# Moving the setup of four second-half rows from the start of a kernel into its groups 2 to 4, with new priorities for the first half

## The chip, the cores and the metric

The kernel runs on one core of one Trainium2 chip. A core has five engines that run side by side: TensorE for matrix products (PE in the profile, PEld for its weight loads), VectorE (DVE), ScalarE (ACT), GpSimd (POOL), and SyncE (SP), whose only work here is to issue DMAs. The metric is the device time of one launch in microseconds (us). The kernel before was run three times, and its median is 2317.83 us (2316.39 to 2319.93).

## What is computed

The input x holds 128 samples of 64 tokens with 512 features, and adj a 64 by 64 matrix for each sample. Four layers follow one another. Each is `x = x + f(relu(layernorm(x)), adj)`, all in float32. The four f, cut to what matters here:

```python
# layer 0: hypergraph convolution, twice, with layer norm between
h = relu(Dn * H @ (Be * H.T @ (x @ W1.T)) + b1);  h = layer_norm(h, gamma, beta)
y = Dn * H @ (Be * H.T @ (h @ W2.T)) + b2 + x
# layer 1: s = (x @ w) @ a decides the attention weights
A = exp(leaky(8 * tanh((s_i + s_j) / 8))) * adj;  y = normalised(A) @ x @ w
# layer 2: query and key with biases, value
y = normalised(adj * exp((x @ Wq.T + bq) @ (x @ Wk.T + bk).T)) @ (x @ Wv.T + bv)
# layer 3: two scores per token, then three powers of a transition matrix
Xw = X @ Wv + bv;  sj = Xw @ aw[:512];  si = Xw @ aw[512:]
T = rownormalised(adj * exp(leaky_relu(sj_j + si_i + ab)))
y = relu(sum over k of (T^k X @ Wk[k] + bk[k]))
```

Two small results of weights alone matter for the change. The first is the column `gb_c`, Wk transposed times bq, which layer 2 adds to its queries. The second is the pair of rows `c3_b[:, s, :]`, Wv times one half of aw, with which layer 3 takes its two scores straight from the normalised x, and with them the scalar `kap` (bv times both halves of aw, plus ab). No layer of the first half reads any of these.

## The kernel before, in words

The 8192 tokens are cut into NG = 16 groups of 512, and a group into four tiles of 128 tokens. The **first half** of the kernel takes every group through layers 0 and 1 (`layer0`, L771; `layer1`, L849) and stores x to DRAM. The **second half** loads it again and takes every group through layers 2 and 3 (`layer2`, L896; `layer3`, L1009). The large products are Strassen products of two by two blocks (`strassen` at L673 and `chained` at L621), so DVE, ACT and POOL have block sums to make between the matmuls. Weights are combined once (`combine` at L395), at the start for the first half, and at the joint of the halves for the second.

The order of the work is not written out. Each step is entered into a `Graph` (L40) with an engine, a cost and a priority, and `Graph.run` (L84) plays the whole program through once with these costs and gives each engine its list of instructions. It takes on each engine the step that can start first, and among steps that can start at the same time the one with the lowest priority number. The number is `G.prio + G.shift`: `G.prio` begins at g * PERIOD1 in the first half, or 16 * PERIOD1 + g * PERIOD2 in the second, and grows along the layer by `step`, stretched by `STRETCH`. `G.shift` is the entry of the table `AT` (L291) for the part named by `part(...)`. So a lower number means earlier, and only differences count. The entries end00, end01 and end11 are added for the last groups: end01 for layer 1 of group 14, end11 for layer 1 of group 15. When the graph foresees over 1 us of idle time on PE, `fill` (L1195) puts in matmuls of `ones` with no use for their result, for half of that time. They are on L1199 in the profile.

Buffers are slots of a tag. A step that needs a new buffer waits until a slot of the tag is free. The tag `tmp` has four slots of 128 by 512, and three kinds of work use it:

- the setup: `setup_l2` (L469, products of Wq and Wk), `setup_l1` (L463, the row `wa_b` for layer 1), `setup_bq` (L486) and `setup_l3` (L503), through `temp` (L341) with its load on L338;
- `spread` (L455), which turns a column into a row on all partitions: a DVE product on L458, a matmul with ones on L460, an ACT copy on L461;
- `transposed` (L597) in layer 0: an ACT copy into a slot (L601), a DMA transpose (L602), and an ACT copy of what came back (L603).

Several tags of the first half hand their memory to tags of the second half once all their steps are done (`TWO`, L197): the block sums `s2` and `s1` to `zz`, `wa` to `q`, `z` to `hT`, `mT` to `sx`.

Before, `setup_bq` and `setup_l3` are entered at the start, after the combinations of the first half's weights. `setup_bq` loads four blocks of Wk, sums them with the entries of bq on DVE (L492, L494), and takes a matmul with ones (L499) and a copy (L501). `setup_l3` does for each s two broadcast loads (aw and bv3) and four loads of Wv, five dot products on DVE (`dot`, L390, on L392), and one `spread`; two small additions (L514, L515) make `kap`. All DMAs are on SP's queue, in one order.

Of the kernel before, what the change touches and what calls it, by code (L numbers as in the profile page):

```python
# [14 lines left out]
P = 128  # L15
C = 64
D = 512
# [154 lines left out]
def tile_adj_preln_d4(  # L172
# [111 lines left out]
    def quad(b):  # L284
# [2 lines left out]
    FILL, LAT = 0.5, 2.3  # L287


    STRETCH, PERIOD1, PERIOD2 = (2.4057, 23.1237, 14.6194, 5.0478), 88.385, 152.83  # L290
    AT = {  # L291
        "x0": -4649.81, "apart": 515.41, "w1": 891.32, "b1": 147.15, "w2": 1055.04, "w": 146.66, "c1": 74.0, "l0":
        181.27, "c2": 131.25, "l1": 1241.14, "c": -4314.2, "g0": -2118.58, "g1": -4213.04, "g2": -574.45, "g3":
        -1827.82, "g": -443.79, "bq": -420.39, "l3": -143.58, "wg": 627.97, "wp": 228.79, "beg0": -1054.79, "beg1":
        -138.73, "end00": 1.09, "end01": -86.62, "end11": 256.44, "new2": -124.9, "new3": 81.75, "end2": -68.63,
        "end3": -133.99, "load1": -63.98, "load2": 661.26, "m": -63.44, "h0": 2.91, "p0": 25.16, "z0": -386.05,
        "q0": 47.65, "y0": -4107.25, "h1": -19.07, "p1": 5.7, "z1": -84.16, "q1": 20.96, "y1": -130.14, "s": -234.6,
        "t0": -462.0, "e0": -467.09, "t1": -348.17, "e1": -282.93, "hT": 524.3, "sh": 245.53, "lq": 730.58, "pt":
        -113.04, "v": 589.88, "pv": 1100.8, "s3": 672.72, "tt": 1008.78, "a0": 690.15, "b0": 538.95, "a1": 811.73,
        "ws": 2002.18, "load3": 441.07, "bk": 299.55,  # L300
    }

    def part(name):
        G.shift = AT[name]
# [28 lines left out]
        dma(8, lambda: nc.sync.dma_start(sb, src), [], [name])  # L333
        return sb

    def load_tmp(tag, n, shape_of, src):
        b = Buf(tag)
        dma(n * P * 4 / 1024, lambda: nc.sync.dma_start(shape_of(b.t), src), [], [b])  # L338
        return b

    def temp(src):  # L341

        return load_tmp("tmp", D, lambda t: t, src)

    xt, adjs, xmid, rows = {}, {}, {}, []

# [136 lines left out]
            act(0.6, lambda c=c, e=e: nc.scalar.copy(e.t, ps[c].t), [ps[c]], [e])  # L483
            dma(256, lambda c=c, e=e: nc.sync.dma_start(wg_d[c * P:(c + 1) * P, :], e.t), [e], ["wg_d"])

    def setup_bq():  # L486

        pg, bk = Buf("ps"), Buf("o")
        for o in range(KD):
            k_ = temp(Wk[o * P:(o + 1) * P, :])  # L490
            if o == 0:
                dvp(0.45, lambda k_=k_: nc.vector.tensor_scalar(bk.t, k_.t, bq_c[:, 0:1], None, op0=ALU.mult), [k_, "bq_c"], [bk])  # L492
            else:
                dvp(0.85, lambda o=o, k_=k_: nc.vector.scalar_tensor_tensor(bk.t, k_.t, bq_c[:, o:o + 1], bk.t, op0=ALU.mult, op1=ALU.add),  # L494
                    [k_, "bq_c", bk], [bk])

        def mg():
            for c in range(KD):
                nc.tensor.matmul(pg.t[:, c:c + 1], bk.t[:, c * P:(c + 1) * P], ones[:, 0:1], start=True, stop=True)  # L499
        pe(c_mm(1, KD), mg, [bk], [pg])  # L500
        dve(0.2, lambda: nc.vector.tensor_copy(gb_c, pg.t[:, :KD]), [pg], ["gb"])  # L501

    def setup_l3():  # L503
        kk = Buf("mv")
        ab_t = load_tmp("rs", 1, lambda t: t, ab.partition_broadcast(P))
        for s in range(2):
            av, cc = temp(aw[s * D:(s + 1) * D].partition_broadcast(P)), Buf("col")
            bv_t = temp(bv3.partition_broadcast(P))
            dot(lambda bv_t=bv_t: bv_t.t, lambda av=av: av.t, lambda s=s: kk.t[:, s:s + 1], [bv_t, av], [(kk, s)])
            for c in range(KD):  # L510
                wv = temp(Wv3[c * P:(c + 1) * P, :])
                dot(lambda wv=wv: wv.t, lambda av=av: av.t, lambda c=c, cc=cc: cc.t[:, c:c + 1], [wv, av], [(cc, c)])
            spread(lambda cc=cc: cc.t, lambda s=s: c3_b[:, s, :], [(cc, c) for c in range(KD)], ("c3", s))
        dve(0.15, lambda: nc.vector.tensor_add(kap, kk.t[:, 0:1], kk.t[:, 1:2]), [(kk, 0), (kk, 1)], ["kap"])  # L514
        dve(0.15, lambda: nc.vector.tensor_add(kap, kap, ab_t.t), ["kap", ab_t], ["kap"])  # L515

# [492 lines left out]
    def layer3(g):  # L1009
# [66 lines left out]


        part("b0")
        sx = Buf("sx")
        keys = lambda i, v: [(a3[2 * i + v], n) for n in range(3)]  # L1080
        block = lambda i, j: [(lambda v=v: a3[2 * i + v].t[:, :, 2 * j:2 * j + 2, :]) for v in range(2)]
# [131 lines left out]
    setup_l1()  # L1213
    part("c")
    W = combine(wm, w_sb, w_x, 2, D // 2, "DVE")
    part("bq")
    setup_bq()
    part("l3")
    setup_l3()
    for g in range(NG):  # L1220
        G.prio = g * PERIOD1
        if g:
            part("load1")
            load_group(g, x_in)
        for i, layer in ((0, layer0), (1, layer1)):
            stretch[0] = STRETCH[i]
            if g == 0:
                G.prio += AT["beg0" if i == 0 else "beg1"]
            if i == 0 and g == NG - 1:
                G.prio += AT["end00"]  # L1230
            if i == 1 and g >= NG - 2:
                G.prio += AT["end01" if g == NG - 2 else "end11"]
            layer(g)
        G.prio = g * PERIOD1
        part("wp")
        if g:
            for k in range(2):
                if 2 * g - 2 + k < 21:
                    setup_w3(2 * g - 2 + k, [("z", g - 1 + k, 1 - k)], [("z", g, k)])
# [83 lines left out]
```

## Time and profile before

| | us |
|---|---|
| median of three runs | 2317.83 |
| lowest and highest | 2316.39, 2319.93 |
| the profiled execution, its own time | 2321.51 |
| its span, first to last instruction | 2319.7 |
| first matmul of layer 0 (L790) starts | 6.28 |
| first product of layer 1 (L691 with 256 columns on mT) starts | 149.68 |
| last product of layer 1 ends | 1223.6 |
| first product of layer 3 (L1124) starts | 1264.30 |

The granted TensorE clock is 0.999 of full speed over the whole execution. Times within the profile count from the span's first instruction. A timeline row has the start, the time from the first to the last of a run of equal instructions, the engine, line and operation, what is written and read, and in brackets the idle time before it with what ended it. A row of a table by stage has the busy time of each engine in a stretch, its instruction count in brackets, the granted clock, the busy share of the DMA engines and the rate of their transfers. A row of waits says which engine's instruction waited for which, for how long in total, how often, and the longest.

### The profile page before, as it was taken

Reading aid. Unit: us, or ns where it says so; the run is one execution under the profiler, and the core shown is the slowest. Engines: PE = TensorE matmul, PEld = TensorE weight load, DVE = VectorE, ACT = ScalarE, POOL = GpSimd, SP = SyncE. Lnnn points to the kernel's source line nnn. Section 1 sums busy time; section 2 is a strip of 40 time slices with the busy share of each in tenths; the row PEclk is TensorE's granted clock in tenths of the full one; section 3 lists DMA queues with packets and bytes.
Section 4 is the critical chain, followed back from the end, with each engine's and each line's share of the span. In section 5 each row is a group of like instructions: output and inputs, shape, how many; then the busy total and the mean of one; then the engine's idle time right before and its main releaser. Section 6 shows DMA issues by size and latency. Waiting matters only on the chain.

```text
span 2319.7 us, 39752 instructions
## 1 busy us (share of the span) xinstructions
PE 2279.9 (98%) x14238; PEld 1866.4 (80%) x14238; DVE 1865.1 (80%) x4004; ACT 1393.2 (60%) x1993; POOL 1190.9 (51%) x1771
## 2 busy tenths in 40 slices
PE   8999999999999999999999999999999999999998
PEld 4676677776777767777688999999999989999898
DVE  7887877887778877787867888888888878788787
ACT  4766565675655765656657566566656655656542
POOL 7445556545665465543433455545455544545443
PEclk9999999999999999999999999999999999999999
DMA  6443233443333342323436877787787877878767
GB/s 232 103 104 77 78 98 79 102 90 79 83 91 94 90 90 58 74 71 68 97 98 161 223 222 229 234 223 213 226 244 213 235 215 217 222 224 225 200 200 242
DMA packets 403478, 355.12 MB, mean 153 GB/s; under 512 B 290896, under 2 KB 321872, under 8 KB 403280
## 3 DMA queue, kind: packets, MB, share of 16 engines
q1 hardware_dynamic: 403280, 352.58, 55.5%
q8 instruction: 112, 1.84, 0.3%
q14 instruction: 86, 0.70, 0.1%
HBM read 241.05 MB, written 44.33 MB: 123 GB/s over the span
## 4 chain that ended last, share of the span: by engine, by line
PE 84%; DMA 6%; DVE 5%; ACT 3%; issue 1%; POOL 1%; SPq 0%; DVEq 0%; ACTq 0%; POOLq 0%
PE ps L691 38%; PE ps L1124 19%; PE ps L930 15%; PE ps L592 4%; PE ps L844 2%; PE ps L1067 2%; DMA w2m_wm_a_wf<-fac 1%; DMA h<-o 1%; PE ps L999 1%; PE ps L961 1%; DMA x<-xm 1%; DMA z_hT<-tmp_mB_xi 1%; ACT h L583 1%; DVE st L562 1%; DMA tmp_mB_xi<-in_Wk_dram 0%
## 5 line engine op out<-in xcount | busy, mean ns | idle before, releaser
L583 ACT ACTIVATE h<-x,nm,rs 128x512 f32<-128x512 f32 x384 | 306.2, 812 | 234.9 <-POOL nm L570 220.3
L564 POOL TENSOR_SCALAR rs<-mv 128x1 f32<-128x1 f32 x320 | 104.6, 327 | 388.4 <-DVE mv L563 371.1
L1124 PE MATMUL ps<-w2m_wm_a_wf 128*128 128x128 f32 x2256 | 295.5, 277 | 3.8 <-DMA w2m_wm_a_wf<-fac 2.2
L1124 PEld LDWEIGHTS ps<-w2m_wm_a_wf 128*128 128x128 f32 x2256 | 275.8, 192 | 11.1 <-issue 4.0
L691 PE MATMUL ps<-w2m_wm_a_wf,s_s_zz 128*128 128x256 f32 x1152 | 274.8, 380 | 1.8 <-DVE s_s_zz L683 1.8
L1124 PE MATMUL ps<-w2m_wm_a_wf,tmp_mB_xi 128*128 128x128 f32 x1968 | 260.4, 277 | 9.8 <-DMA w2m_wm_a_wf<-fac 5.2
L1124 PEld LDWEIGHTS ps<-w2m_wm_a_wf,tmp_mB_xi 128*128 128x128 f32 x1968 | 243.2, 193 | 16.6 <-ACT h L583 7.5
L691 PEld LDWEIGHTS ps<-w2m_wm_a_wf,s_s_zz 128*128 128x128 f32 x1152 | 217.7, 190 | 39.7 <-issue 9.6
L691 PE MATMUL ps<-w2m_wm_a_wf,rT_vu_tt 128*128 128x256 f32 x1024 | 237.5, 380 | 2.0 <-ACT row_sh L453 0.7
L691 PE MATMUL ps<-wa_mem,mT_sx 128*128 128x512 f32 x512 | 238.1, 593 | 1.3 <-DMA wa_mem<-in_W1T_dram 1.0
L691 PEld LDWEIGHTS ps<-w2m_wm_a_wf,rT_vu_tt 128*128 128x128 f32 x1024 | 193.6, 190 | 48.5 <-issue 18.4
L565 POOL TENSOR_TENSOR rs<-rs,mhalf 128x1 f32<-128x1 f32 x320 | 209.2, 654 | 26.5
L562 DVE BATCH_NORM_STATS2 st<-x 128x6 f32<-128x512 f32 x256 | 176.1, 688 | 33.0 <-DMA x<-xm 25.7
L570 POOL TENSOR_SCALAR nm<-mv,rs 128x1 f32<-128x1 f32 x320 | 171.4, 537 | 30.2
L691 PE MATMUL ps<-wa_mem,s_s_zz 128*128 128x512 f32 x384 | 180.3, 593 | 0.0
L691 PEld LDWEIGHTS ps<-wa_mem,mT_sx 128*128 128x128 f32 x512 | 96.0, 191 | 103.9 <-issue 97.9
L818 ACT ACTIVATE z_hT<-z_hT 128x512 f32<-128x512 f32 x128 | 79.3, 630 | 133.6 <-DVE z_hT L711 133.6
L603 ACT COPY rT_vu_tt<-z_hT 128x1024 uint16<-128x1024 uint16 x128 | 146.7, 1162 | 16.6 <-DMA z_hT<-tmp_mB_xi 16.5
L719 POOL TENSOR_TENSOR u<-u,row_sh 128x256 f32<-128x256 f32 x96 | 75.4, 794 | 157.3 <-DVE u L661 134.7
L592 PEld LDWEIGHTS ps<-bd,h 128*128 128x128 f32 x1024 | 126.6, 192 | 36.4 <-issue 27.6
L885 POOL TENSOR_TENSOR x<-x,u 128x256 f32<-128x256 f32 x96 | 88.8, 950 | 113.0 <-DVE u L663 113.0
L601 ACT COPY o<-h 128x1024 uint16<-128x1024 uint16 x128 | 133.8, 1047 | 9.3 <-DVE h L1056 6.9
(205 smaller groups left out, 4991.8 us busy)
## 6 DMA issues: line engine op xcount, KB each, us to landing
w2m_wm_a_wf<-fac SPq DMA_DIRECT2D x110, 768.0 KB, 5.0
w2m_wm_a_wf<-fac SPq DMA_DIRECT2D x109, 576.0 KB, 4.8
x<-xm SPq DMA_DIRECT2D x128, 256.0 KB, 3.5
x<-in_x_dram SPq DMA_DIRECT2D x64, 256.0 KB, 2.8
xm<-x SPq DMA_DIRECT2D x64, 256.0 KB, 2.0
out_dram<-x SPq DMA_DIRECT2D x64, 256.0 KB, 3.9
adj<-in_adj_dram SPq DMA_DIRECT2D x32, 256.0 KB, 4.6
fac<-wp_bv_bk SPq DMA_DIRECT2D x63, 128.0 KB, 2.0
```

The lines of the kernel that those rows point to most:

```text
L562: dve(0.69, lambda i=i: nc.vector.bn_stats(st.t[:, i, :], src(i)), [r[i]], [(st, i)])
L564: small(0.28, lambda: nc.gpsimd.tensor_scalar_add(rs.t, mv.t[:, 1:2], EPS), [mv], [rs])
L565: small(0.62, lambda: nc.gpsimd.tensor_tensor(rs.t, rs.t, mhalf, ALU.pow), [rs], [rs])
L570: small(0.32, lambda: nc.gpsimd.tensor_scalar(nm.t, mv.t[:, 0:1], rs.t, -1.0, op0=ALU.mult, op1=ALU.mult), [mv, rs], [nm])
L583: act(0.82, lambda: nc.scalar.activation(h.t, xx.t, AF.Relu, bias=nm.t, scale=rs.t), [xx, nm, rs], [h])
L592: nc.tensor.matmul(quad(p)[:, c, :], h.t[:, c * P:(c + 1) * P], rhs(), start=True, stop=True)
L601: act(1.05, lambda: nc.scalar.copy(u16(planes.t).rearrange("p (q c) -> p q c", q=2), u16(src()).rearrange("p (c q) -> p q c", q=2)), ksrc, ...
L603: act(1.16, lambda: nc.scalar.copy(u16(dst()).rearrange("p c (k q) -> p c k q", q=2), u16(back()).rearrange("p (q c r) -> p c r q", q=2, c ...
L691: nc.tensor.matmul(p.t[:, :n], lhs()[:, c, :], rhs(c), start=first and c == 0, stop=c == kc - 1, skip_group_check=True)
L885: pool(0.78, lambda: nc.gpsimd.tensor_add(xx.t[:, cols], xx.t[:, cols], U.t[:, iu]), [xx, u], [xx])
L930: nc.tensor.matmul(pair(p.t)[:, o, :], a, b, start=first and o == 0 and c == 0, stop=c == 1, skip_group_check=True)
L1124: nc.tensor.matmul(inner(p, q)[:, r, :], at()[:, k, :], wv()[:, r, k, :], start=first and r == 0 and k == 0, stop=k == 2, skip_group_check ...
```

## The change

`setup_bq` and `setup_l3` are no longer called at the start. They are called in the loop over the groups of the first half, after the layers of the group are entered: `setup_bq` in group 2, and the two halves of `setup_l3` in groups 3 and 4. Their loads get one more entry in their list of reads, `("z", g, 0)`. This names the last step of the layer norm of the first pair of tiles in layer 0 of that group (the `offset` on L570). It stands for no memory: the graph alone knows it, and the built program has no semaphore for it. Between groups 3 and 4 one slot of `mv` and one of `rs` (each has ten) stay taken, for the sums of `kap`.

STRETCH of layers 0 and 1, PERIOD1, and most of the entries in `AT` for the setup and the first half have new values. Those that belong to the second half (new2, new3, end2, end3, load2, hT, sh, lq, pt, v, pv, s3, tt, a0, b0, a1, ws, load3, bk, and wg) are the same. Two new entries, late3 and last3, are added to the priority in layer 3 of the last two groups; both are 0.

```diff
-    STRETCH, PERIOD1, PERIOD2 = (2.4057, 23.1237, 14.6194, 5.0478), 88.385, 152.83
+    STRETCH, PERIOD1, PERIOD2 = (2.5476, 23.631, 14.6194, 5.0478), 89.881, 152.83
     AT = {
-        "x0": -4649.81, "apart": 515.41, "w1": 891.32, "b1": 147.15, "w2": 1055.04, "w": 146.66, "c1": 74.0, "l0":
-        181.27, "c2": 131.25, "l1": 1241.14, "c": -4314.2, "g0": -2118.58, "g1": -4213.04, "g2": -574.45, "g3":
-        -1827.82, "g": -443.79, "bq": -420.39, "l3": -143.58, "wg": 627.97, "wp": 228.79, "beg0": -1054.79, "beg1":
-        -138.73, "end00": 1.09, "end01": -86.62, "end11": 256.44, "new2": -124.9, "new3": 81.75, "end2": -68.63,
+        "x0": -3955.4, "apart": 260.05, "w1": 1321.68, "b1": 557.01, "w2": 2258.25, "w": 829.09, "c1": -850.87,
+        "l0": -579.26, "c2": 1820.29, "l1": 854.76, "c": 115.55, "g0": -2147.26, "g1": -2547.69, "g2": -40.9, "g3":
+        -1911.72, "g": -569.47, "bq": 23.11, "l3": -4.68, "wg": 627.97, "wp": 228.79, "beg0": -1894.5, "beg1":
+        -468.39, "end00": -12.24, "end01": -489.71, "end11": 597.53, "new2": -124.9, "new3": 81.75, "end2": -68.63,
...
-    def load_tmp(tag, n, shape_of, src):
+    def load_tmp(tag, n, shape_of, src, r=()):
         b = Buf(tag)
-        dma(n * P * 4 / 1024, lambda: nc.sync.dma_start(shape_of(b.t), src), [], [b])
+        dma(n * P * 4 / 1024, lambda: nc.sync.dma_start(shape_of(b.t), src), r, [b])
...
-    def setup_bq():
+    def setup_bq(when):
...
-            k_ = temp(Wk[o * P:(o + 1) * P, :])
+            k_ = temp(Wk[o * P:(o + 1) * P, :], when)
...
-    def setup_l3():
-        kk = Buf("mv")
-        ab_t = load_tmp("rs", 1, lambda t: t, ab.partition_broadcast(P))
-        for s in range(2):
...
+    def setup_l3(s, when):
+        if not s:
+            sums.append((Buf("mv"), load_tmp("rs", 1, lambda t: t, ab.partition_broadcast(P), when)))
+        kk, ab_t = sums[0]
+        av, cc = temp(aw[s * D:(s + 1) * D].partition_broadcast(P), when), Buf("col")
+        bv_t = temp(bv3.partition_broadcast(P), when)
+        dot(lambda: bv_t.t, lambda: av.t, lambda: kk.t[:, s:s + 1], [bv_t, av], [(kk, s)])
+        for c in range(KD):
+            wv = temp(Wv3[c * P:(c + 1) * P, :], when)
+            dot(lambda wv=wv: wv.t, lambda: av.t, lambda c=c: cc.t[:, c:c + 1], [wv, av], [(cc, c)])
+        spread(lambda: cc.t, lambda: c3_b[:, s, :], [(cc, c) for c in range(KD)], ("c3", s))
+        if not s:
+            return
...
-    part("bq")
-    setup_bq()
-    part("l3")
-    setup_l3()
+    sums = []
     for g in range(NG):
...
+        if g in (2, 3, 4):
+            part("bq" if g == 2 else "l3")
+            when = [("z", g, 0)]
+            setup_bq(when) if g == 2 else setup_l3(g - 3, when)
+            part("wp")
```

## Prediction

> **What bounds the kernel now.** I read the page first, then busy time by stage, then TensorE's timeline where a stage shows idle time, then the waits there. The page:
>
> ```profile
> span 2319.7 us, 39752 instructions
> PE 2279.9 (98%) x14238; PEld 1866.4 (80%) x14238; DVE 1865.1 (80%) x4004; ACT 1393.2 (60%) x1993; POOL 1190.9 (51%) x1771
> ```
>
> TensorE is the bound, and 2319.7 - 2279.9 = 39.8 us is all it is idle. Its products are the same before and after, so the time can change by idle time and by the filler matmuls on L1199, which count as busy and are not work. Stages of 58 us show where that is (the second column is PE's busy time; the rows are the first four, one from the steady part, and three at the joint of the halves):
>
> ```profile
> 0.00:58.00 58.00, 51.11 (x204) 28.57 (x205) 41.58 (x88) 26.19 (x42) 41.10 (x59) 1.00 0.67 232
> 58.00:116.00 58.00, 55.17 (x209) 36.51 (x208) 51.67 (x103) 41.91 (x58) 25.11 (x35) 1.00 0.43 103
> 116.00:174.00 58.00, 56.29 (x275) 43.89 (x274) 48.56 (x114) 36.64 (x50) 26.93 (x44) 1.00 0.42 104
> 174.00:232.00 58.00, 57.63 (x246) 39.34 (x245) 45.21 (x100) 39.42 (x53) 30.61 (x51) 1.00 0.35 78
> ...
> 406.00:464.00 58.00, 58.00 (x258) 42.53 (x257) 47.30 (x108) 36.12 (x51) 29.68 (x48) 1.00 0.41 101
> ...
> 1160.00:1218.00 58.00, 58.00 (x335) 50.75 (x335) 39.17 (x85) 31.47 (x49) 19.57 (x31) 1.00 0.37 99
> 1218.00:1276.00 58.00, 54.52 (x415) 48.57 (x415) 44.55 (x106) 42.68 (x61) 21.39 (x42) 1.00 0.64 162
> 1276.00:1334.00 58.00, 57.44 (x485) 53.08 (x483) 48.24 (x105) 31.51 (x48) 27.52 (x40) 1.00 0.82 222
> ```
>
> The first four stages lose 6.89 + 2.83 + 1.71 + 0.37 = 11.8 us; a steady one loses nothing. In the second, DVE is busy 51.67 of 58 (89%; 47.30, 82%, in the steady part). The timeline of TensorE shows the fillers, and the two largest losses after the first 31 us:
>
> ```profile
> 97.93 1.50 PE L1199 MATMUL ps<-ones 128*128 128x128 f32 x12
> 100.65 2.00 PE L691 MATMUL ps<-w2m_wm_a_wf,s_s_zz 128*128 128x256 f32 x8 [1.22 <-DVE s_s_zz L683]
> ...
> 139.55 1.73 PE L1199 MATMUL ps<-ones 128*128 128x128 f32 x14
> 141.20 1.98 PE L844 MATMUL ps<-y_qT,bd 128*128 128x512 f32 x4
> 143.02 2.17 PE L1199 MATMUL ps<-ones 128*128 128x128 f32 x18
> 146.90 2.94 PE L592 MATMUL ps<-bd,h 128*128 128x128 f32 x24 [1.71 <-DVE bd L873]
> ```
>
> All fillers of the start take 2.93 + 1.65 + 1.50 + 1.73 + 2.17 = 9.98 us there (the first two runs, at 1.04 and 7.34, aren't shown). Lost at the start, then: 11.8 + 9.98 = 21.8 us. Of this 6.28 us pass before the first real matmul, 2.88 us at 7.34 wait for a load of Wk, 1.16 at 24 for another, 0.98 at 30 for W1. The rest is 2.72 at 97.93 (to 100.65), 1.65 and 3.88 = 5.5 around 139 to 147, and some 2.2 in six small waits. What the moved setup does there, by DVE's group and by the waits up to 160 us:
>
> ```profile
> L392 DVE SCALAR_TENSOR_TENSOR o<-tmp_mB_xi x10: 636/687/1637, 64.8 to 92.5; 128x512 f32<-128x512 f32 x10
> ACT tmp_mB_xi L601 <- DVE o L392: 2.8, 3, 1.5
> SPq L338 <- DVE o L392: 9.1, 3, 5.5
> ```
>
> Ten dot products lie between 64.8 and 92.5, and three times a copy ahead of a transpose (L601) waits until one of them gives its `tmp` slot back. SP's queue stands 9.1 us on the loads, with the transposes behind them.
>
> **What the Trainium skill says.** "Perfetto Trace Analysis", section Identifying the Most-Contended Engine, holds that a busy TensorE isn't a TensorE near its limit; the section Optimization Strategy after it adds that a kernel can have regimes with different limits. The trace agrees: the fillers are busy time without work, and the start has another regime than the steady part. "SBUF — State Buffer", section Two separate sides, says that GpSimd and VectorE share a port pair, which one locks for a whole instruction, also when the DVE operation has two SBUF inputs and GpSimd reads SBUF. The dots have two SBUF inputs: their median is 687 ns and their longest 1637, the one at 69.67, while POOL's addition from 69.16 runs. That agrees.
>
> **The change part by part.** *Taken from the start, DVE:* setup_bq has 0.49 + 1.64 + 0.74 + 0.70 + 0.16 us between 56.7 and 64.8, 3.7 us; setup_l3 has ten dots of 8.8 us together, their accumulator reads of 0.8 (ten of 0.08), two diagonal products of 0.68 and two additions of 0.15, 11.3 us. That is 15.0 us out of the 38 us from 57 to 95, in which DVE is the engine nearest its limit. *SP and DMA:* 16 loads of 256 KB and one small one go from the start (all but `ab`, at 5.67, issued from 51.3 on). The loads that the early losses wait for are ahead of them, so those waits don't go with the move itself. *PE and ACT:* matmuls of 0.95 + 2 x 1.02 = 3.0 us and two copies of 0.58 move and cost PE the same later.
>
> *What that frees.* The stall at 97.93 ends with a block sum that waits, through copy, transpose and norm, on DVE's and the slots' work between 85 and 99; with 3.7 us less of dots, reads and a diagonal product in front (2.68 + 0.32 + 0.68) it should go: 2.7 us at most. The stall at 139 to 147 is layer 1's first chain: the row `wa_b` lands at 127.67 + 0.59 = 128.3, its load was issued at 98.9 behind the loads of Wv. The last x that the chain needs is ready at 121.66 + 0.75 = 122.4, so the chain can move up by some 5 us at most, if the row no longer is last; then its norms are. I count 3.5 of 5.5. Of the six small waits, 2.2 us, half: 1.1. The new order of the start (new numbers for nearly every part) can also reach some of the 2.88 + 1.16 + 0.98 = 5.0 us of load waits, but these loads already share DMA stages of up to 335 GB/s (20 to 40 us), and the x and weights still come in; I count 1.0, bounds -2 to +4. Sum: 2.7 + 3.5 + 1.1 + 1.0 = 8.3 us gained.
>
> *Added in groups 2 to 4.* A group takes (372.0 - 227.3) / 2 = 72.4 us there by its first matmuls. DVE gets 2.75 us in group 2 (0.49 + 3 x 0.70 + 0.16) and 5 x 0.77 + 0.68 = 4.5 in groups 3 and 4, on 0.82 x 72.4 = 59; it stays at 88% or less, as loaded as the stage of 58 to 116 was. Slots of `tmp`: eight transposes a group hold one for about 1.05 + 1.24 + 3.1 = 5.4 us, 43 of 4 x 72.4 = 290 slot-us; six loads and a product more don't fill it. On SP the loads stand in line with transposes, stores of x and the rows of layer 1; each issue is 0.33 to 0.43 us, and the graph places a load where it sees a free slot; a load that stands too long holds the transposes behind it. The read of ("z", g, 0) adds no wait on the chip. Cover: TensorE has ready products of three groups; if that cover were gone, a late load would cost its landing, 2.7 us, once per group, so 0 to 8. I take 0.5. The slots of `mv` and `rs` held for a group, one of ten: nothing, since the norms use them in turn and DVE is ahead.
>
> *The steady groups* lose next to nothing (58.00 of 58.00), so new numbers can't gain there, only lose: 0 to 3, I take 0.
>
> *The joint.* Its two stages lose 3.48 + 0.56 = 4.04 us and hold fillers of 1.28 + 1.95 + 1.28 = 4.5, 8.5 in all. The second half's numbers are kept, but its neighbour's aren't: layer 1 of group 14 comes earlier by 403 (end01 -86.62 to -489.71), that of group 15 later by 341 (end11 256.44 to 597.53). Counted from the joint's origin, 16 * PERIOD1, by hand (57.1 us of layer 0's steps and 10.6 of layer 1's, each times its STRETCH, plus end00, end11 and e1, less PERIOD1), the last Strassen product of group 15's layer 1 began at 270 and now begins at 581, beside layer 2's query products of group 0 at 611, which stood behind it. It can so fill their gaps, or end later and keep layer 3 of group 0 waiting for the memory it holds. The trace of before can't decide; I bound it by -5 (most of 8.5) and +12, and take 0.
>
> Sum: -8.3 + 0.5 + 0 + 0 = -7.8 us. Against the profiled execution, 2321.51 (1.8 around the span of 2319.7), that is 2313.7. The median of the runs lies 3.7 below that execution, which gives 2310.0.
>
> **The rivals.** *The start is bound by its chains, not by DVE.* TensorE has nothing to do at 139 because layer 0 of the first groups must end first, and a DVE with less to do only idles more; the stall moves along. Then 97.93 goes and little else, 2.7 - 0.5, near -2: 2315.8. For it: PE's early waits are for loads; against it: DVE's 89% and the slot waits. *The joint runs dry (slower).* The last product of layer 1 ends at 1223.6 and the first of layer 3 comes at 1264.3, 41 us later, covered by layers 2. Group 15's layer 1 is 14 products of 0.86 us = 12.1 us, plus 2.68 + 0.89 = 3.6 for its 32 matmuls on L592. If it ends later by d while layer 2 of group 0 is used up before, up to d is bare, since `zz`, `q` and `sx` are its memory. At 7.8 + 4.6 = 12.4 it is slower by 0.2%; at the whole 15.7, the sum is +7.9: 2325.7. For it: a number moved by 341 with the second half's unmoved. Against it: PE takes what is ready, so a late number alone doesn't delay work while nothing else is ready. *The fuller gain:* all of 10.4 us of later stalls, 2 of the load waits and 4 of the joint, -16: 2302. *It doesn't do what it says:* the loads would still be early if their numbers put them there; the reads of ("z", g, 0) rule that out.
>
> **How the numbers follow.** Likeliest, 2310.0, own range 2304 to 2315: 0.58. Chains, 2315.8: 0.20. Joint dry, from 2322 up: 0.14. Fuller gain, about 2302: 0.08. A measurement of this kernel can tell about 0.2%, 4.6 us, from no change: faster is below 2313.2, slower above 2322.5. Faster: 0.52 of the likeliest, 0.08 of the fuller gain, 0.05 of the chains, 0.65. Slower: 0.15. Same: 0.20. The range 2302 to 2321 leaves out most of the dry joint and the edge of the fuller gain.
>
> **What would show it.** Right: no dots on `tmp` before 150 us; L601 without waits on L392; the row `wa_b` earlier than 128 us; PE's idle plus fillers in the first 232 us at 13 to 14 instead of 21.8; stages between 232 and 464 still within 1 us of full; 8 to 9 us lost at the joint. Wrong: a start that loses over 18 us; waits of PE on DVE or on transposes in groups 2 to 4; over 12 us of idle time and fillers between 1150 and 1340; or a second half whose waits on DMA differ by more than 3 us.

## The result, and the profile after

The changed kernel takes 2311.16 us (median of six runs, 2308.01 to 2315.08); the kernel before took 2319.41 beside it on the same chip (2316.39 to 2320.2). The ratio is 0.9966 [0.9954, 0.9978]. The profiled execution took 2313.18. The forecast was 2310.0: the number and the sign hold. Where the time came from does not, as the rest shows.

The page of the changed kernel: span, TensorE, and one of its DMA queues (kind, packets, MB, share of 16 engines).

```profile
span 2311.4 us, 39694 instructions
...
PE 2276.7 (99%) x14200; PEld 1859.7 (80%) x14200; DVE 1872.4 (81%) x4004; ACT 1395.1 (60%) x1993; POOL 1187.5 (51%) x1771
...
q8 instruction: 112, 1.84, 0.3%
```

TensorE is idle for 34.7 us instead of 39.8, and runs 38 matmuls less, all of them fillers. (A filler of the program shows as two matmuls in the trace: 138 before and 100 after are 69 and 50 of the program's, and the expectations below count the program's.) So 5.1 us of idle time are gone and 5.5 us of fillers (20.09 to 14.61 in the group of that line). The table by stage (same columns as in the prediction: PE's busy time, then PEld, DVE, ACT, POOL, clock, DMA share, GB/s):

```profile
0.00:58.00 58.00, 50.71 (x200) 27.67 (x201) 38.94 (x88) 29.68 (x46) 42.11 (x60) 0.94 0.64 223
58.00:116.00 58.00, 55.28 (x198) 36.68 (x197) 47.79 (x87) 40.09 (x54) 24.30 (x37) 0.97 0.27 55
116.00:174.00 58.00, 56.23 (x265) 42.79 (x264) 47.09 (x107) 35.19 (x49) 30.20 (x47) 1.00 0.39 103
174.00:232.00 58.00, 57.18 (x259) 41.26 (x258) 47.44 (x104) 39.26 (x55) 28.07 (x48) 1.00 0.44 97
...
406.00:464.00 58.00, 57.98 (x257) 42.15 (x256) 48.45 (x109) 36.49 (x51) 30.34 (x47) 1.00 0.41 101
...
1218.00:1276.00 58.00, 54.96 (x419) 48.95 (x418) 45.03 (x107) 43.09 (x61) 22.14 (x43) 1.00 0.63 164
1276.00:1334.00 58.00, 57.16 (x482) 52.62 (x481) 47.83 (x103) 31.01 (x47) 26.42 (x40) 1.00 0.80 221
```

DVE is less busy in the second stage, 47.79 instead of 51.67, as it should be. But the first four stages still lose 7.29 + 2.72 + 1.77 + 0.82 = 12.6 us of idle time (before: 11.8). Their fillers fall from 9.98 to 4.00 + 2.39 = 6.4. That is 19.0 us instead of 21.8; 13 to 14 was forecast, and over 18 was named as a sign against it. The joint loses 3.04 + 0.84 and has 4.5 of fillers, 8.4: as before.

TensorE's timeline of the changed kernel shows why the start gives little (stalls and fillers between 61 and 192 us):

```profile
65.70 3.58 PE L693 MATMUL ps<-w2m_wm_a_wf,rT_vu_tt 128*128 128x256 f32 x8 [2.22 <-ACT u L661]
...
119.92 2.39 PE L1203 MATMUL ps<-ones 128*128 128x128 f32 x20
123.61 1.99 PE L693 MATMUL ps<-w2m_wm_a_wf,rT_vu_tt 128*128 128x256 f32 x8 [1.31 <-ACT rT_vu_tt L605]
...
191.13 1.05 PE L499 MATMUL ps<-ones,o 128*128 128x1 f32 x8 [0.82 <-DVE o L494]
```

The stalls at 97.93 and at 139 to 147 are gone. In their place are one at 63 to 65 (a Strassen chain that waits for ACT's copy), one at 120 to 123 (a transpose's copy), and one at 190, where the moved setup itself keeps TensorE waiting. The first has a second price: 8 matmuls of 256 columns take 3.58 us at 65.70 and 1.99 at 123.61.

**Where the time came from.** To place it, I use one measure for all traces, the *lost time* at a point: the time of the point, less what the matmuls begun by then need at their usual spacing (0.429 us for 512 columns, 0.216 for 256, 0.111 for 128, narrower ones at theirs); fillers count as nothing. The two kernels do the same 2217.8 us of matmuls. For two profiles of each:

```
lost time, us, at      58   116   150   232   406  1220  1340  1900  2200  2300
before               14.7  20.5  26.5  27.5  29.4  34.5  46.6  66.3  82.2  94.6
before, once more    15.1  20.9  27.0  28.1  30.3  36.2  47.5  69.6  85.2  96.1
after                13.8  18.8  22.6  25.3  28.5  34.3  46.4  66.5  74.0  86.7
after, once more     13.0  18.0  22.1  24.9  28.5  36.2  47.4  68.2  77.4  90.0
```

The new start is 4 to 5 us ahead at 150, 2 to 3 at 232, and level at 1220, the end of the first half. All of the gain that lasts, 6 to 8 us, comes in the second half, between 1900 and 2200: 15.9 and 15.6 us are lost there before, 7.5 and 9.2 after.

That is where the change does nothing: compared from the end and without fillers, the last 9132 matmuls are the same ones in the same order in both traces, and so are the last instructions of the other engines, from about 1234 us on at the latest. TensorE enters this part at the same time, 1183.12 before and 1182.84 after. What differs is when DMAs are issued and when they land. TensorE's waits from 1334 us to the end, in the kernel before:

```profile
PE ps L1124 <- DMA w2m_wm_a_wf<-fac: 7.8, 8, 1.7
PE ps L1124 <- DVE x L1005: 2.7, 1, 2.7
PE ps L930 <- ACT z_hT L603: 1.7, 3, 0.8
```

and in the kernel after (total, times, longest):

```profile
PE ps L1128 <- DMA w2m_wm_a_wf<-fac: 5.9, 7, 1.9
PE ps L932 <- ACT z_hT L605: 0.9, 2, 0.6
```

`fac` is the table of combined weights, read back from DRAM for layer 3; three loads of 576 to 768 KB go with each group. Before, three of the stalls stand 138 us apart, at the first product of a group's layer 3:

```profile
1889.86 1.58 PE L1124 MATMUL ps<-w2m_wm_a_wf,tmp_mB_xi 128*128 128x128 f32 x12 [1.74 <-DMA w2m_wm_a_wf<-fac]
...
2027.73 1.58 PE L1124 MATMUL ps<-w2m_wm_a_wf,tmp_mB_xi 128*128 128x128 f32 x12 [0.77 <-DMA w2m_wm_a_wf<-fac]
...
2166.78 2.42 PE L1124 MATMUL ps<-w2m_wm_a_wf,tmp_mB_xi 128*128 128x128 f32 x12 [2.68 <-DVE x L1005]
```

After, the same twelve matmuls start at once in the first two places:

```profile
1890.45 1.50 PE L1128 MATMUL ps<-w2m_wm_a_wf,tmp_mB_xi 128*128 128x128 f32 x12
...
2025.76 1.50 PE L1128 MATMUL ps<-w2m_wm_a_wf,tmp_mB_xi 128*128 128x128 f32 x12
```

The third stall is put down to an addition on DVE, which ends at 2166.66; the first of the factor loads issued from 2160.91 on lands at 2166.65, so both came last. It is followed by slow matmuls (2.42 us instead of 1.50). Measured as the excess over the usual spacing, the three make 5.7 us before and 0.3 after. (The 6.7 us that an expectation below gives for them seems to take in the slow matmuls of the third.) Of the 8.4 us that 1900 to 2200 differ by, two of them make 3.8, the slow matmuls 1.7, and a wait of 1.0 at 2105 for a transposed z the next part; the rest is in waits of less than 1 us. The DMA groups of the stretch 1878 to 1892, before:

```profile
w2m_wm_a_wf<-fac SPq DMA_DIRECT2D x2, 576.0 KB, 6.5
w2m_wm_a_wf<-fac SPq DMA_DIRECT2D x1, 768.0 KB, 7.0
```

and after (last number: median us from issue to landing):

```profile
w2m_wm_a_wf<-fac SPq DMA_DIRECT2D x2, 576.0 KB, 4.5
w2m_wm_a_wf<-fac SPq DMA_DIRECT2D x1, 768.0 KB, 4.3
```

As a group the loads take 2 to 3 us less; the first of the three, for which TensorE waits, takes 4.9 us before and 4.0 after. Why?

### The profile page after: what moved, and what is told of

Its sections match the earlier page's. It is cut to its first block, busy times and chain, and to the rows that moved or that the text cites. A ratio compares the mean times of both kernels' runs of the same rounds, so it can differ in the third digit from the quotient of the medians.

```text
span 2311.4 us, 39694 instructions
## 1 busy us (share of the span) xinstructions
PE 2276.7 (99%) x14200; PEld 1859.7 (80%) x14200; DVE 1872.4 (81%) x4004; ACT 1395.1 (60%) x1993; POOL 1187.5 (51%) x1771
## 3 DMA queue, kind: packets, MB, share of 16 engines
q8 instruction: 112, 1.84, 0.3%
## 4 chain that ended last, share of the span: by engine, by line
PE 87%; DMA 5%; DVE 4%; ACT 2%; POOL 1%; issue 1%; SPq 0%; DVEq 0%; ACTq 0%; POOLq 0%
PE ps L693 40%; PE ps L1128 19%; PE ps L932 15%; PE ps L594 5%; PE ps L846 2%; PE ps L1069 2%; PE ps L1001 2%; DMA w2m_wm_a_wf<-fac 2%; PE ps L963 1%; DMA h<-o 1%; DMA x<-xm 1%; DMA out_dram<-x 1%; DMA tmp_mB_xi<-in_Wk_dram 1%; PE ps L477 1%; ACT h L585 0%
## 5 line engine op out<-in xcount | busy, mean ns | idle before, releaser
L693 PE MATMUL ps<-w2m_wm_a_wf,rT_vu_tt 128*128 128x256 f32 x1024 | 242.3, 382 | 4.5 <-ACT u L661 2.7
L572 POOL TENSOR_SCALAR nm<-mv,rs 128x1 f32<-128x1 f32 x320 | 183.8, 575 | 29.9
L1137 ACT COPY s_s_zz<-ps 128x384 f32<-128x384 f32 (+1 forms) x128 | 68.1, 532 | 117.8 <-PE ps L1128 115.0
```

The source lines that it names most:

```text
L572: small(0.32, lambda: nc.gpsimd.tensor_scalar(nm.t, mv.t[:, 0:1], rs.t, -1.0, op0=ALU.mult, op1=ALU.mult), [mv, rs], [nm])
L693: nc.tensor.matmul(p.t[:, :n], lhs()[:, c, :], rhs(c), start=first and c == 0, stop=c == kc - 1, skip_group_check=True)
```

## Theories

The prediction's theory was that DVE is relieved at the start. After the result it can stand only if the start's gain is somehow kept to the end; its rival is that the second half itself runs differently. For the second half's cause I had three theories (A, B and C in the expectations; in those of the first four runs, theory 1 places the gain in the second half and theory 2 in the first). **A, the place of the buffers:** the same steps run, but x, h, o and a few small tags get other slots, since the first half leaves them free in another order. **B, instruction loads:** the engines' programs are read by DMA during the run, TensorE's in blocks of 16 KB (queue q8 above). "Runtime: NRT & Kernel Launch", section Instruction fetch mechanics, gives 16 KiB blocks of 256 instructions, fetched by the sequencer through a queue of its own, at a cost it calls mostly hidden. The trace agrees on the size: 112 loads are 1.84 MB, 16.4 KB each. With 38 fillers fewer in the trace, 76 instructions fewer (each has a weight load), the blocks end 0.3 of a block earlier in the order of the work, and may no longer fall on the same factor loads. **C, the joint's handover:** the first half passes memory and data on at other moments, and the second half keeps that offset.

## The experiments

Ratios are to the kernel before in the same call; its median moved between 2321.8 and 2324.2 from call to call.

**The kernel before, once more** (no edit).

> The kernel before once more, for a second trace. Lost time is taken as the time of a point of the trace less the TensorE work done up to it (each matmul at its steady spacing: 0.429 us for 512 columns, 0.216 for 256, 0.111 for 128). In the first trace it is 27.5 us at 232 us, 34.5 at 1220 and 94.6 at 2300. Theory 1 (the gain lies in the second half and belongs to the program): again 34 to 35 at 1220 and 93 to 96 at 2300, ratio 1.000. Theory 2 (the gain lies in the first half and the first pair of traces hid it, by half-clock stretches in the changed kernel and by chance in the second half): 34 to 36 at 1220, but the second half some 5 to 8 us below the 60 us of the first trace.

Measured: 1.0003 [0.9993, 1.0013]; second half 59.9 us lost (60.1 in the first trace), with 15.6 between 1900 and 2200. So the pattern is the kernel's own and not that of one execution.

**The changed kernel, once more** (no edit).

> The changed kernel once more, for a second trace. In the first trace lost time is 25.3 us at 232, 34.3 at 1220, 86.7 at 2300. Theory 1: 33 to 35 at 1220 and 51 to 53 us in the second half again. Theory 2: without the half-clock stretches of the first trace 30 to 32 at 1220, and a second half of 52 to 60.

Measured: 0.9962 [0.9947, 0.9976], second half 53.8. The three stalls sum to 0. A new one of 2.4 us stands at 1685. The gain repeats, in the same stretch.

**The move alone**, with the numbers of before except the two of the moved parts:

```diff
-    STRETCH, PERIOD1, PERIOD2 = (2.5476, 23.631, 14.6194, 5.0478), 89.881, 152.83
+    STRETCH, PERIOD1, PERIOD2 = (2.4057, 23.1237, 14.6194, 5.0478), 88.385, 152.83
...
-        "x0": -3955.4, "apart": 260.05, "w1": 1321.68, "b1": 557.01, "w2": 2258.25, "w": 829.09, "c1": -850.87,
+        "x0": -4649.81, "apart": 515.41, "w1": 891.32, "b1": 147.15, "w2": 1055.04, "w": 146.66, "c1": 74.0, "l0":
...
```

> The setup of the four rows in groups 2 to 4, with all priorities of the kernel before (bq and l3 at their new numbers, 23.11 and -4.68). Theory 1 (the gain is a second half that happens to wait less for its factors): no fixed sign; lost time at 1220 near 34, the second half anywhere between 52 and 60 us. Theory 2 (the gain is in the first half): by the prediction's steps about 6 us less lost at 232 than the 27.5 of before, so some 2312 us, ratio 0.997; if the new numbers are needed for it, 26 to 28 lost at 232 and ratio 0.999 to 1.002.

Measured: 1.0015 [1.0006, 1.0023]. Its start is the best of these at 150 us (21.9 lost; before 26.5), only 1 ahead at 232 (26.6), and behind at 1220 (42.5; before 34.5): 5.4 us lost between 232 and 406 and 10.5 from there to the joint, where before loses 1.9 and 5.1. The second half loses 55.4, five less than before (three less over the same matmuls; see the table of all traces). So the move alone does free the start, and the later groups pay for it; the new numbers are what keeps groups 2 to 15 from that.

**The numbers alone**, with the setup at the start:

```diff
-        -1911.72, "g": -569.47, "bq": 23.11, "l3": -4.68, "wg": 627.97, "wp": 228.79, "beg0": -1894.5, "beg1":
+        -1911.72, "g": -569.47, "bq": -420.39, "l3": -3000, "wg": 627.97, "wp": 228.79, "beg0": -1894.5, "beg1":
...
+    part("bq")
+    setup_bq([])
+    part("l3")
+    for s in range(2):
+        setup_l3(s, [])
...
-        if g in (2, 3, 4):
...
```

> The new priorities with the setup still at the start (bq at -420.39 as before; l3 at -3000, because with other numbers the four tmp slots don't suffice for an order). Theory 1: first half 1 to 4 us longer than before, second half anywhere between 52 and 60 us of lost time, so a ratio of 0.997 to 1.002. Theory 2: the dots are back among the first 100 us; lost time at 232 is 27 us or more, and the ratio 0.999 to 1.003.

Measured: 1.0163 [1.0146, 1.018]. 64.2 us are lost by 232, twice the loss of before. Its waits of TensorE up to 60 us start with a row made by `spread`:

```profile
PE ps L460 <- DVE tmp_mB_xi L458: 4.4, 1, 4.4
```

The new numbers don't bear the setup in front of them; its own start number for l3 (-3000) may be part of that loss, so this is no clean "numbers only". Its second half, entered about 44 us later, loses 48.7 between the same times as before's 60, but its last 44 us then fall outside; over the same matmuls it loses some 7 less than before. A gain in the second half thus doesn't need the setup to be moved.

**Buffers in another place.** Every tag's list of slots is reversed, in both kernels:

```diff
+    for tag in (*SLOTS, "ps"):
+        slots[tag].reverse()
```

> The kernel before with the same order on every engine, but every tag of plain slots and the PSUM banks in reverse: slot 0 of x is where slot 8 was, and so on. The two traces of before and the two of the changed kernel give the second half (from 1220 us on) 60.1, 59.9, 52.4 and 53.8 us of lost time with the same order of instructions there and other slots of x, h, o, bd and PSUM. Theory A (the place of the buffers decides): the second half moves by 3 us or more from 60, ratio 0.996 to 0.999 or over 1.001. Theory B (it is the fetch of instructions, whose loads fall on other points of the program): 59 to 61 us, ratio 1.000 within 0.001. Theory C (what the joint hands over decides): 59 to 61 as well.

> The changed kernel with the same reversal of slots. Theory A: the second half moves from 52 to 54 us of lost time to 55 or more, ratio 0.998 or more to before. Theories B and C: 52 to 54, ratio 0.996 to 0.997.

Measured: 0.9992 [0.9985, 1.0] and 0.996 [0.9944, 0.9975]. The traces lose 56.2 and 47.7 in the second half, four to six less than without the edit, but the executions profiled are some 3 and 1 us below their medians, and the medians hardly move. Places do change stalls one by one (at 1889.9: 1.03 instead of 1.90 us), and the traces moved by more than A asked for, the changed kernel's the other way; but by the medians places don't make the difference between the two kernels. A falls as the main cause.

**No fillers**, in both kernels:

```diff
-    FILL, LAT = 0.5, 2.3
+    FILL, LAT = 0.0, 2.3
```

> The kernel before with none of its 69 filler matmuls: the program of TensorE is shorter from the start on, so its instruction loads fall elsewhere, the order and the slots of all else are the same. Theory B: the second half moves by 3 us or more from 60 us. Theories A and C: within 2 us of 60 up to 2160 us. In either case, if idle time without fillers costs clock, half-clock stretches after 6, 143 and 1235 us, up to 1.7 us each, ratio 1.000 to 1.002.

> The changed kernel with none of its filler matmuls. Theory B: the second half moves by 2 us or more from 52 to 54 us. Theories A and C: 52 to 54, ratio to before 0.996 to 0.998, with half-clock stretches at the start as in its own trace (7.5 and 65.5 us).

Measured: 0.9976 [0.9967, 0.9985] and 0.9956 [0.9941, 0.9971]. By 1220 the kernel before has lost the same without them (36.0). Its second half has lost 54.0 instead of 60: removing matmuls that feed nothing gains some 5 us (the medians differ by 5.1), and by the trace all of it beyond 1220, although stretches of half clock came as foreseen, at 147 and 1239 us. In the changed kernel it moves nothing that can be told (0.9962 before the edit). The distance between the two kernels shrinks to 0.2%.

**Fillers that cross the two over.** By B, a number of fillers exists at which the kernel before has its instruction loads off the three factor loads, and one at which the changed kernel has them on. Counting instructions gave 0.15 for the one and 0.25 for the other:

```diff
-    FILL, LAT = 0.5, 2.3
+    FILL, LAT = 0.15, 2.3
```

> The kernel before with its fillers cut from 0.5 to 0.15 of the foreseen gap: 42 matmuls fewer before 1220 us (14 of 56 stay), order and slots else the same. A TensorE instruction load (16 KB, queue q8) holds 256 instructions, 64 of these matmuls, so 42 fewer move the points where loads fall by a third of their distance, to about 6 us before and 8 us after the first factor load ahead of the stalls at 1889.9, 2027.7 and 2166.8, where the changed kernel has them. Theory B (an instruction load that falls on a factor load makes it late): these three stalls shrink from 6.7 us together (5.7, 6.2 and 4.3 in the other old-order traces) to under 4, the second half from 60 to 53 to 56, ratio 0.996 to 0.998. Theory C (the joint hands over something else): the three stalls stay near 5 us.

> The changed kernel with its fillers cut from 0.5 to 0.25: 20 matmuls fewer before 1220 us (17 of 37 stay), which puts TensorE's instruction loads 1 to 2 us ahead of the first factor load, where the kernel before has them. Theory B: the stalls at the places of 1889.9, 2027.7 and 2166.8 come back, 2 us or more together (0.3 and 0.0 in its two traces), less than before's, because the loads of the other engines (q14) are elsewhere; second half 53 to 57. Theory C: under 0.5 us together, second half 50 to 54.

Measured: 1.0 [0.999, 1.0009] and 0.999 [0.9982, 0.9997]. The three stalls do cross: 1.9 us instead of 5.7 in the first, 3.6 instead of 0.3 in the second. But the whole doesn't follow for the first: new stalls stand elsewhere, 1.9 us at 1556 among them, and its second half loses 57.9. TensorE's waits after 1334 us there, eight factor waits grown to thirteen:

```profile
PE ps L1124 <- DMA w2m_wm_a_wf<-fac: 9.3, 13, 1.6
```

In the second, the changed kernel with half the fillers, they are

```profile
PE ps L1128 <- DMA w2m_wm_a_wf<-fac: 6.0, 9, 1.7
PE ps L1128 <- DVE s_s_zz L1147: 3.1, 2, 2.2
PE ps L1128 <- DVE x L1007: 2.4, 2, 1.8
```

and its second half loses 58.2, nearly as much as before, though its start is the best of all (22.7 at 232). It keeps 0.1% of a gain of 0.4%. So the gain of the change hangs on how many useless matmuls the program holds: 0.9962 with FILL at 0.5, 0.999 at 0.25, 0.9956 at 0, each against the kernel before at 0.5. B, as it was put, is weakened too: in the second trace the instruction loads start 4.8 to 5.7 us ahead of the factor loads, close to their place in the changed kernel (6.1 to 7.0) and not on top of them, as the count had them, and the stalls came all the same.

**Without the two setups.** Their rows are set to zero on DVE in both kernels, so this part of the computation is left out:

```diff
-        pg, bk = Buf("ps"), Buf("o")
-        for o in range(KD):
...
+        dve(0.2, lambda: nc.vector.memset(gb_c, 0.0), [], ["gb"])
...
+            dve(0.3, lambda s=s: nc.vector.memset(c3_b[:, s, :], 0.0), [], [("c3", s)])
+        dve(0.15, lambda: nc.vector.memset(kap, 0.0), [], ["kap"])
...
```

> The kernel before without the work of setup_bq and setup_l3: gb_c, c3_b and kap are set to zero, so layers 2 and 3 don't get their rows. It prices what the setup costs at the start. The prediction's step: 6 to 9 us less lost at 232 than 27.5. The rival of the chains: 1 to 3 us less at 232, and 34 less 3 of its own matmuls' slack at 1220, so no less than 32.

> The changed kernel without the work of setup_bq and setup_l3 (the same three set to zero in groups 2 to 4). It prices what the setup costs there. The prediction's step: 0.5 us less lost between 174 and 406 than the changed kernel's 4.4 to 5.0 us. If the moved work costs more there: 1.5 us or more less, and a lost time at 1220 of 32 or less instead of 34 to 36.

Measured: 0.9987 [0.9979, 0.9994] and 0.9948 [0.9934, 0.9961]. In the kernel before, the setup costs 5.1 us by 100 (20.0 to 14.9) and 6.1 by 150 (26.5 to 20.4), and then only 2 to 3 by 232 (27.5 and 28.1 to 25.3); by 1220 nothing is left (37.7). From 150 to 232 it loses 4.9 us without the setup and 1.0 with it: a stall behind `bd`, like the one that stood at 146.90, is now found 68 us later, with 1.9 us of fillers before it.

```profile
214.94 2.94 PE L567 MATMUL ps<-bd,h 128*128 128x128 f32 x24 [1.36 <-DVE bd L848]
```

In the changed kernel, the lost time between 232 and 406 is no smaller without the setup (5.6 instead of 3.2 and 3.6), so the moved setup costs nothing there that could be measured. The three stalls are gone from the kernel before here too (0.3 us), but its second half still loses 59.5: the three stalls are one form of the loss and not its cause.

All traces together, ordered by the lost time of the second half:

```
                 lost at   lost at   1220 to  1900 to  2200 to  second   three
                 232       1220      1900     2200     2300     half     stalls
before           27.5      34.5      31.8     15.9     12.4     60.1     5.7
before, again    28.1      36.2      33.4     15.6     10.9     59.9     4.8
before_nosetup   25.3      37.7      37.2      8.2     14.1     59.5     0.3
after_f25        22.7      34.5      33.5      9.9     14.8     58.2     3.6
before_f15       29.9      38.2      37.1      7.7     13.1     57.9     1.9
before_slots     27.3      34.9      31.4     13.3     11.5     56.2     5.6
move_only        26.6      42.5      30.3     13.9     11.2     55.4     5.9
before_nofill    28.8      36.0      30.9     10.8     12.3     54.0     4.3
after, again     24.9      36.2      32.0      9.2     12.6     53.8     0
after            25.3      34.3      32.2      7.5     12.7     52.4     0.3
after_nofill     26.2      35.3      27.8      9.8     12.9     50.5     2.4
after_nosetup    23.4      38.6      29.4      8.2     11.5     49.1     0
numbers_only     64.2      78.2      27.2     12.3      9.2     48.7     0.5
after_slots      28.3      37.9      29.2      7.1     11.4     47.7     0
```

Each is one profiled execution; most executions of a kernel lie within some 3 us of its median. The columns are taken at fixed times, and two kernels enter the second half later, `move_only` by 8 us and `numbers_only` by 44. Over the same matmuls instead (from the point with 1100 us of matmul work left to the last matmul) the loss is 57.9 and 58.4 us before, 54.6 in `move_only`, 50.2 and 51.7 after, and 50.6 in `numbers_only`.

**What the traces say on B.** In ten traces (before, after and the eight kernels up to the fillers' removal) I compared each DMA of the second half with the same DMA in the other traces, by whether instruction loads start between 1 us before and 3 us after its issue:

```
us later than the mean of the same DMA     none     one     two
factor loads                              -0.06    0.16    0.37
x loads                                   -0.14    0.32    0.35
transposes of h                           -0.14    0.13    0.30
stores of the output                      -0.14    0.28    0.38
```

So an instruction load nearby goes with a landing 0.2 to 0.5 us later. "DMA: Bandwidth & Descriptors", section Queues, rings and completion order, says that each DMA engine takes turns, packet by packet, between the queues that have work; that fits, but no run here takes instruction loads away to show it. Ahead of 1889.9, 2027.7 and 2166.8 TensorE's loads start 1.4 and 0.6 us before and 0.3 after the issue of the first factor load in the kernel before, and 6.1 to 7.0 us before it in the changed one. But 0.4 us isn't 1.9, and over the ten traces the summed lateness goes with the second half's loss only loosely (a correlation of about 0.5). It is one push among several.

**What holds up the three factor loads** is for the most part that they are issued later. They stand in SP's one queue behind the transpose of an h; that waits for ACT's h, and the h for the layer norm of an x tile whose load was issued 14 to 16 us before the product. Ahead of 1889.9, in the kernel before, DVE waits for the x and ACT then for the norm; in the changed kernel (last line) ACT waits less:

```profile
1878.48 0.69 DVE L562 BATCH_NORM_STATS2 st<-x 128x6 f32<-128x512 f32 x1 [1.37 <-DMA x<-xm]
...
1881.53 0.81 ACT L583 ACTIVATE h<-x,nm,rs 128x512 f32<-128x512 f32 x1 [2.87 <-POOL nm L570]
...
1881.90 0.81 ACT L585 ACTIVATE h<-x,nm,rs 128x512 f32<-128x512 f32 x1 [0.76 <-POOL nm L572]
```

The table gives the range over the three places in two traces of each kernel; "ahead" is counted back from the moment when TensorE is free for the product:

```
us                        x: issue     x lands    fac is issued   fac: issue    TensorE
                          to landing   ahead      ahead           to landing    idle
before, before again      5.1-6.2       9.6-10.4  3.1-3.7         3.9-5.7       0.4-2.7
after, after again        3.2-4.6      10.7-11.7  4.1-5.4         3.9-4.3       0.0-0.1
```

On the mean the issue is 1.8 us later before (3.3 us ahead instead of 5.1), and the load itself 0.7 us longer (4.8 instead of 4.1). Over all 14 traces, 42 places, TensorE is never idle where the first factor load is issued 4.8 us ahead or more (17 places), and always where it is 4.5 or less (25).

B comes in one step earlier than I had looked for it. The x load takes 4.6 to 6.2 us where a TensorE instruction load starts within 2.5 us after its issue (10 of the 42), and 3.1 to 4.7 where none starts within 3 us (26); the six between lie on both sides (3.2 or 5.2 to 5.3). In the kernel before one starts 1.3 to 2.8 us after it at all six places; in the changed kernel only at the middle place, 2.6 us after it, when the x has nearly landed. The fillers move these loads, and the x loads follow: 3.4 to 3.7 us in the kernel before at 0.15, with none beside them. But there, as in the changed kernel at 0.25 (3.5 to 4.2), the x loads are issued later against TensorE's work (14.1 to 14.4 us ahead, instead of 15.0 to 15.8 in the kernel before), and most of the stalls stay. That the instruction loads make the x loads late is thus an association that follows the fillers; no run takes them away.

**What stays open** is what decides how the second half as a whole falls. A change of the first half's numbers, of the slots, of the setup or of the fillers each moved its loss, between 47.7 and 60.1 us, with TensorE's order in it unchanged (in `numbers_only` two neighbouring DVE instructions near 2031 us are swapped). The fillers don't settle C: at 0.25 the changed kernel loses about as much as the kernel before at 0.5, but the kernel before wasn't run at 0.25. A kept offset isn't seen, though: against TensorE's work, ACT's instructions stand within 0.01 us of each other before and after from 1310 to 1350 us, 0.6 us later before from 1870 to 1910, and level again (0.2 at most) from 1910 to 1950. Of the 15.4 us that TensorE waits after 1334 us in the kernel before, 10.5 end with a factor load, in the changed kernel 5.9 of 9.8. That small shifts of other DMAs make or remove these stalls in general is argued, and not shown; the chain above was followed at three places only. A second half with its x and factor loads issued earlier would tell it, and wasn't tried.

## Why the prediction was right or wrong

That the number was right is luck: the largest term of the sum was wrong and one term was missing, and the two errors nearly cancel. The premise that the time can change only by idle time and fillers also leaves out the clock: after the first 15 us, the profiled run before has one stretch of half clock of 3.4 us (at 2167.3) and that of the changed kernel two (65.5 and 1345.5).

- *"What that frees", 8.3 us: the step that failed.* The two stalls named did go: in the stage of 116 to 150 us, 3.8 us are lost instead of 6.0. But by 232 only 2.2 (and 3.2 in the second pair of traces) of the 8.3 are left, and at 1220 nothing. In the changed kernel the wait has moved on to the next links of the chain, a copy on ACT and a transpose. That was the first rival's mechanism, the chains of layer 0, with its size (2); the kernel before without the setup, whose numbers are unchanged, shows it too. Even without any setup the kernel before has 25.3 us lost at 232. The three things I read as the limit (DVE at 89%, copies waiting for `tmp`, SP's queue) were relieved; none was what TensorE waited for in the end.
- *The signs of the move* are there: the ten dots on `tmp` run from 261.7 on, no copy of `transposed` waits for them any more, and SP's loads of the setup stand 2.4 us for them instead of 9.1. In the changed kernel:

```profile
L392 DVE SCALAR_TENSOR_TENSOR o<-tmp_mB_xi x10: 678/691/926, 261.7 to 341.3; 128x512 f32<-128x512 f32 x10
```

- *The row `wa_b`* is ready at 92.0 + 0.56 us instead of 128.3, as said. The mechanism at 139 to 147 was right and the gain there too, 2.2 of the 3.5; it is given back by 232.
- *Load waits, 1.0 gained:* measured, the first wait for Wk grew from 1.23 to 2.36 us, the second fell from 1.16 to 0.95, and the one for W1 is gone (0.98). By these waits about nothing; yet by 58 us the changed kernel has lost 0.9 us less, and 2.1 in the second pair, so the size fits and the way doesn't.
- *Groups 2 to 4, +0.5:* between 232 and 406 the changed kernel loses 3.2 us against 1.9: +1.3, inside the 0 to 8. Waits of TensorE on DVE, named as a sign against it, came twice, 0.8 us at 190 and 0.6 at 321; the kernel before has two as well (0.6 and 0.4).
- *Steady groups, 0:* from 406 to 1220, 5.8 against 5.1, and 7.7 against 5.9 in the second pair; 1 to 2, inside 0 to 3.
- *The joint, 0:* from 1220 to 1340, 12.1 us in each. Right; the dry joint didn't come, and the entry of the second half stayed within 0.3 us.
- *The second half: no term.* I had given it nothing because its numbers are kept. It brought 6 to 8 us, the whole gain. The sign for it, "a second half whose waits on DMA differ by more than 3 us", was in the list: by name the waits on factor loads differ by 1.9 us (7.8 to 5.9), with the one of 2.7 that ends with a factor load by 4.6, and all waits of TensorE there by 15.4 - 9.8 = 5.6.

No version that computes everything clearly beats the changed kernel: without fillers it has 0.9956 [0.9941, 0.9971], with its slots reversed 0.996 [0.9944, 0.9975].

## What to carry to other kernels

Relieving a busy engine at the start of a long kernel gives only what is left some stages later: follow the lost time (time less matmul work done) to the end of the stage, and not to the end of the stall. A second half with the same instructions in the same order can still take 12 us more or less, when its loads have little lead. When a load is late, look first at when it was issued and at what stood ahead of it in its queue. A change of 0.3% by new priorities needs a control, such as another filler count in both kernels, before it is put down to its idea. A term set to nothing because "nothing changes there" needs bounds as the others do.

## What the runs showed of the hardware

**A short stall can halve TensorE's clock for a while.** In the changed kernel, in steps of 4 us (PE's busy time, clock, DMA share, GB/s):

```profile
61.00:65.00 4.00, 1.99 (x8) 1.00 0.05 9
65.00:69.00 4.00, 3.30 (x8) 0.57 0.83 176
69.00:73.00 4.00, 4.00 (x12) 1.00 0.03 11
```

The stall of 2.22 us before 65.70 is followed by half the clock for 3.4 us, at a cost of 1.7 us, which a table of busy time hides. The same follows the 2.68-us stall at 2164 in the kernel before. "TensorE: Matmul & The Clock Gate", section What's actually happening, has this state come after an idle window of about 3.4 us; here 2.2 us were enough, and the length of the slow stretch, 3.4 us, agrees with its window. The length of a stall alone doesn't decide. In the clock records of the 14 traces, from 15 us on, every half-clock stretch begins on a fixed grid of 3.41 us. Where TensorE is idle for 2.0 us or more of one step of the grid, the next step is always slow (19 steps); with 1.66 to 1.96 us idle 4 of 28 are, with less none. A stall of 2.59 us at 1236.9 in the kernel before without the setups falls on two steps, with 1.96 us in one of them, and costs no clock.

**Instruction loads** show as a queue of their own, one block of 16 KB for TensorE about every 15 us in the second half (the median distance is 15.2 to 15.9 us in ten traces, single ones 7 to 25), and the data DMAs issued beside one land later, as the tables above have it.
